# Graph attention on one Trainium2 core: one shared weight tile for the last chunk of six heads, 0/1 patterns for 17 of 22 chunks, and exponentials taken per node

## The chip, the core and the metric

The kernel runs on one core of a Trainium2 chip. The metric is device time in microseconds (us) of one execution, the median of several. The engines are named as in the profile: PE is the TensorE matrix engine (PEld its weight loads), DVE is VectorE, ACT is ScalarE, POOL is GpSimd, and SP is SyncE, which here only issues DMAs.

## The reference, cut to what matters

Four graph layers run one after the other on 2708 nodes with 512 features and a dense 0/1 adjacency of 2708 x 2708. Each layer is `x = x + layer(relu(layernorm(x)), adj)`. Only layer 2 is touched. It is masked attention with eight heads of 64 features:

```python
Wh = jnp.einsum('nd,hdo->hno', x, W)
f1 = jnp.einsum('hno,ho->hn', Wh, a1)
f2 = jnp.einsum('hno,ho->hn', Wh, a2)
e = jax.nn.leaky_relu(f1[:, :, None] + f2[:, None, :], negative_slope=ALPHA)   # 0.2
e = jnp.where(adj[None, :, :] > 0, e, NEG_INF)
attention = jax.nn.softmax(e, axis=-1)
h_prime = jnp.einsum('hnm,hmo->hno', attention, Wh)
out = jax.nn.elu(h_prime)
```

The kernel never forms `e`. For a node n and a neighbour m, exp(leaky(f1+f2)) equals e^(f2) * e^(0.2 f1) * max(e^(0.8 f1), e^(-0.8 f2)). The factor e^(0.2 f1) belongs to n alone and cancels in the softmax. So the kernel needs three things: `rb`, the row of e^(0.8 f1) over all n, the same on every partition; `ec`, one number e^(-0.8 f2) for each m; and `ef`, one number e^(f2) for each m, which is multiplied into the rows of Wh.

## The kernel before

**Chunks, units and steps.** The neighbours m are cut into NC = 22 chunks of R = 128 rows. The last one, chunk 21, has only 20 rows (`last_rows`). The columns n of one head are a *unit*. Heads 1 to 6 are whole units of 2708 columns (units 2 to 7). Head 0 is cut into two units of 1408 and 1300 columns (units 0 and 1), and so is head 7 (units 8 and 9). A *step* is one chunk of one unit: 10 x 22 = 220 steps, unit by unit, in each the chunks 0 to 21.

**What one step does.**

- `make` (L979) runs on DVE. One instruction gives the tile of weights t = max(rb, ec) * vT, where vT is the adjacency in bytes: 128 x 2708 numbers, or 20 x 2708 for the last chunk. The tiles t rotate through a ring of four buffers.
- `scale` (L967) runs on ACT. It makes the other operand, `whs` = Wh * ef (64 columns), and for most steps a second small tile for the sums of the weights (32 columns, L975).
- `multiply` (L1180) runs on PE. It adds t times whs into the PSUM tiles `av`, and into the PSUM tiles `sums` the sums of the weights, as float32 matmuls.
- `compare` (L996) and `multiply_sides` (L1195) replace those float32 sums in part of the steps. In units 2 to 8, for the chunks in the list `BY_SIDE`, ACT turns t into a bfloat16 pattern b of zeros and ones: a Sigmoid with the slope 2^62 says which side of the max was taken. PE multiplies b with small precomputed `parts`. The rest of the sum doesn't depend on the side, and is had from a count of neighbours that is made once for all heads.
- `mask` (L1250) and `count_neighbors` (L1258) make that count. For each chunk in `BY_SIDE` ACT casts the bytes of vT to bfloat16 in four pieces (tiles `x`, a ring of five that other tiles share), and PE multiplies them. These casts are laid among the steps of units 0 and 1, two steps for one chunk.
- `evict` (L1205) copies a finished unit from PSUM on ACT, and SP issues the DMAs to DRAM (`avT`, `sumT`).

`BY_SIDE` has 13 chunks before: `m % 5 in (1, 3, 4)`.

**Rows and exponentials.** f1 and f2 of all nodes lie in `f12`, nodes on partitions. `row2` (L1060) turns f1 of one chunk round on PE (`f_ps`), ACT copies it and issues its DMA to `rT` in DRAM. `load_row1` (L934) reads a row of rT back by DMA onto all 128 partitions (1354 KB for 2708 columns), and `exp_row` (L944) takes its exponential on ACT, once for each unit of the head, or half of it. `exps2` takes the exponentials `ef` and `ec`. `exp_nodes` (L1287) takes e^(0.8 f1) again in node layout into `er`, for layer 3. The calls of `row2` for chunks 0 to 16 and the first row of rb come with the dense product that ends before the attention (`rows2`, L1074). Those for chunks 17 to 21 come in the first steps of unit 0.

**Order of the work.** The program writes the steps in one loop (L1338): with step s it writes `scale` and `make` of step s+3, `compare` of step s+1, `multiply` of step s, `multiply_sides` of step s-1, and then what `plan` has for s, entered by `behind(step, function, ...)`. A scheduler then orders the instructions on each engine anew, within what the data and the rings allow, so the order on an engine can differ from the order of the program. [...]

Of the kernel before, what the change touches and what calls it, by code (L numbers as in the profile page):

```python
# [8 lines left out]
F32 = mybir.dt.float32  # L9
# [5 lines left out]
AF = mybir.ActivationFunctionType  # L15
ALU = mybir.AluOpType
# [4 lines left out]
P = 128  # L21

R = 128
# [7 lines left out]
SLOPE2 = 0.2  # L31
# [13 lines left out]
def fast_layers(  # L45
# [36 lines left out]
    nc = tc.nc  # L82
    N, D = x_in.shape
    H, _, O = w2.shape
    NC = -(-N // R)
# [3 lines left out]
    last_rows = N - (NC - 1) * R  # L89
    assert last_rows <= TAIL and TAIL + last_rows <= R  # L90

    def rows(c):
        return min(R, N - c * R)
# [18 lines left out]
    EARLY = NC // 2  # L112
# [14 lines left out]
    ident = const.tile([P, P], F32, name="ident")  # L127
# [274 lines left out]
    vT = []  # L402
# [5 lines left out]
    where = {c: (g, k) for g, cs in enumerate(groups) for k, c in enumerate(cs)}  # L408
# [481 lines left out]

    BY_SIDE = [m for m in range(NC) if m % 5 in (1, 3, 4)]


    STEEP = 2.0**62
# [5 lines left out]
    units[-1:] = [(H - 1, 0, cut), (H - 1, cut, N)]  # L902
    units[:1] = [(0, 0, cut), (0, cut, N)]
    assert all((hi - lo) % 4 == 0 for _, lo, hi in units)
    steps = [(u, m) for u in range(len(units)) for m in range(NC)]

    def by_side(u, m):
        return 1 < u < len(units) - 1 and m in BY_SIDE
# [6 lines left out]
    late = ctx.enter_context(tc.tile_pool(name="late", bufs=1))  # L915
    f12 = late.tile([P, NC, 2 * H], F32, name="f12")
    nc.gpsimd.memset(f12, 0.0)
    at_ctx = ctx.enter_context(ExitStack())
    at = at_ctx.enter_context(tc.tile_pool(name="att", bufs=1, reuse_waits="tile"))
    ef = at.tile([R, NC, H], F32, name="ef")  # L920
# [8 lines left out]
    one6 = at.tile([R, S], F32, name="one6")  # L929
    nc.gpsimd.memset(one6, 0.0)  # L930
    nc.gpsimd.memset(one6[:, 6:7], 1.0)
    row, weight, wh, whs, acc, sides, made, scaled = {}, {}, {}, {}, {}, {}, [], []

    def load_row1(h, lo, hi):  # L934

# [5 lines left out]
            bass.AP(tensor=src.tensor, offset=src.offset, ap=[[0, R], [1, hi - lo]]),  # L941
        )

    def exp_row(h, lo, hi):  # L944
        t = row[h][:, lo:hi]

        with tc.issue_after(scaled[-1]) if scaled else ExitStack():
            nc.scalar.activation(t, t, AF.Exp, scale=1.0 - SLOPE2)


    GROUP = 3

    def load_wh(s):
        u, m = steps[s]
        h = units[u][0]
        t = at.tile([R, GROUP, O], F32, name="wh", bufs=3)
        k = min(GROUP, NC - 1 - m)
        if k > 0:
            src = whd[m * R : (m + k) * R, h * O : (h + 1) * O]
            nc.sync.dma_start(t[:, :k], src.rearrange("(k p) o -> p k o", p=R))  # L960
        if k < GROUP and m + k == NC - 1:
            src = whd[(NC - 1) * R :, h * O : (h + 1) * O]
            nc.sync.dma_start(t[:last_rows, k], src)
        for j in range(GROUP):
            wh[u, m + j] = t[:, j]

    def scale(s):  # L967

        u, m = steps[s]
        h, q = units[u][0], rows(m)  # L970
        t = at.tile([R, O + S], F32, name="whs", bufs=4)
        by = ef[:q, m, h : h + 1]
        ins = nc.scalar.activation(t[:q, :O], wh.pop((u, m))[:q], AF.Copy, scale=by)  # L973
        if not by_side(u, m):
            nc.scalar.activation(t[:q, O:], one6[:q], AF.Copy, scale=by)  # L975
        whs[s] = t
        scaled.append(ins.ins)

    def make(s):  # L979
        u, m = steps[s]  # L980
        h, lo, hi = units[u]
        q = rows(m)
        g, k = where[m]
        t = at.tile([R, N], F32, name="t2", bufs=TILES)
        ins = nc.vector.scalar_tensor_tensor(  # L985
            t[:q, : hi - lo],
            row[h][:q, lo:hi],
            ec[:q, m, h : h + 1],
            vT[g][:q, k, lo:hi],
            op0=ALU.max,  # L990
            op1=ALU.mult,
        )
        weight[s] = t
        made.append(ins.ins)

    def compare(s):  # L996

        u, m = steps[s]
        h, lo, hi = units[u]
        q = rows(m)  # L1000
        if by_side(u, m):
            b = at.tile([R, N], BF16, name="b", bufs=2)
            nc.scalar.activation(  # L1003
                b[:q, : hi - lo],
                weight[s][:q, : hi - lo],
                AF.Sigmoid,
                bias=eb[:q, m, h : h + 1],
                scale=STEEP,
            )
            sides[s] = b  # L1010
# [48 lines left out]

    def row2(c):  # L1060
        pf = ps.tile([P, R], F32, name="f_ps", tag="ps")
        nc.tensor.transpose(pf[:H], f12[:R, c, :H], ident[:R, :R])
        r = at.tile([H, R], F32, name="row", bufs=2)
        nc.scalar.copy(r, pf[:H])
        nc.scalar.dma_start(rT[:, c * R : (c + 1) * R], r)

    def exps2(cs):
        nc.scalar.activation(ef[:, cs], f12[:R, cs, H:], AF.Exp)
# [1 line left out]


    LATE = NC - 5

    def rows2(c):  # L1074
        if c < LATE:
            row2(c)
        if c == EARLY - 1:
            load_row1(*units[0])

        if c == LATE:  # L1080
            exps2(slice(0, EARLY))
            exp_row(*units[0])
            load_wh(0)
            load_wh(GROUP)
        if LATE < c <= LATE + 3:
            scale(len(made))
            make(len(made))
# [5 lines left out]
    staged(NC, *stages2, done=len(AHEAD))  # L1093
    l2p.close()

    e3_ctx = ctx.enter_context(ExitStack())
    e3 = e3_ctx.enter_context(tc.tile_pool(name="e3", bufs=2, side="right", reuse_waits="tile"))
    er = e3.tile([R, NC, H], F32, name="er", bufs=1)
    kept3, l3_weights = {}, []


# [77 lines left out]

    def multiply(s):  # L1180
        u, m = steps[s]
        q = rows(m)
        half, quarter = sizes_of(u)
        if m == 0:
            acc[u] = [
                [ps.tile([P, 512], F32, name=name, tag="ps") for _ in pieces(w)]
                for name, w in (("av", half), ("sums", quarter))
            ]
        t, w = weight.pop(s)[:q], whs.pop(s)[:q]
        cols = [w[:, a : a + S] for a in range(0, O + S, S)]  # L1190
        four(acc[u][0], half, [(cols[j % 2], t, j // 2) for j in range(4)], s)
        if not by_side(u, m):
            four(acc[u][1], quarter, [(cols[2], t, j) for j in range(4)], s)
# [26 lines left out]
    def split():  # L1220

        nc.scalar.mul(eb, ec, -STEEP * ABOVE)
        rest = common.tile([P, D], F32, name="rest", tag="t", bufs=3)
        rest = rest[:R, : NC * H].rearrange("p (m h) -> p m h", h=H)
        for i in range(2):
            e = ef
            if i:
                nc.vector.tensor_tensor(rest, ec, ef, ALU.mult)
                e = rest
            for k in range(3):  # L1230
                part = parts_of[:, :, :, 3 * i + k]
                nc.scalar.copy(part, e)
                if k < 2:
                    nc.vector.tensor_tensor(rest, e, part, ALU.subtract)
                    e = rest
        for i, heads in enumerate((slice(1, H), slice(1, H - 1))):
            for r in sorted({m % 5 for m in BY_SIDE}):
                ms = [m for m in BY_SIDE if m % 5 == r]
                src = parts_of[:, r :: 5, heads, 3:6]
                at_i = [BY_SIDE.index(m) for m in ms]  # L1240
                nc.scalar.copy(parts2[:, at_i[0] : at_i[-1] + 1 : 3, i, heads], src)


    fourths = [0, cut // 2, cut, (cut + N) // 2, N]
# [39 lines left out]
                    sumT[7 * H :, fourths[j] + a : fourths[j] + b], t[own, : b - a]  # L1284
                )

    def exp_nodes():  # L1287
        nc.scalar.activation(er, f12[:R, :, :H], AF.Exp, scale=1.0 - SLOPE2)
        nc.sync.dma_start(er[TAIL : TAIL + last_rows, NC - 1], er[:last_rows, NC - 1])

    def load_l3_weights():
# [6 lines left out]
    def behind(s, fn, *args):  # L1298
        plan.setdefault(s, []).append((fn, args))

    for c in range(LATE, NC):
        behind(c - LATE + 1, row2, c)
    behind(4, exps2, slice(EARLY, NC))
    behind(5, load_row1, *units[1])
    behind(6, exp_row, *units[1])
    behind(9, split)
    behind(30, load_l3_weights)
    behind(30, exp_nodes)
    for u in range(2, len(units)):
        if units[u][1] == 0:  # L1310
            s = max(1, u - 1) * NC
            behind(s + 2, load_row1, units[u][0], 0, N)
            behind(s + 9, exp_row, units[u][0], 0, N)
    for u in range(len(units)):
        behind((u + 1) * NC - 1, evict, u, 0)
        behind(min((u + 1) * NC, len(steps) - 1), evict, u, 1)
    for i in range(len(BY_SIDE)):
        for j in range(4):
            behind(11 + 2 * i + j // 2, mask, i, j)
        behind(13 + 2 * i, count_neighbors, i)  # L1320

    for at_step, fn, c in (
        (16, load3, 0),
# [12 lines left out]
        behind(len(steps) - at_step, fn, c)  # L1336

    for s in range(len(steps)):  # L1338
        if s + 6 < len(steps) and (s + 6) % NC % GROUP == 0:
            load_wh(s + 6)  # L1340
        if s + 3 < len(steps):
            scale(s + 3)
            make(s + 3)
        if s + 1 < len(steps):
            compare(s + 1)
        multiply(s)
        multiply_sides(s - 1)
        for fn, args in plan.pop(s, ()):
            if fn in (load_l3_weights, exp_nodes, split):
                with tc.issue_after(made[s]):  # L1350
                    fn(*args)
            else:
                fn(*args)
# [740 lines left out]
```

## Time and profile before

| what | value |
|---|---|
| median of three runs | 1788.5 us (1788.35 to 1793.66) |
| the profiled execution's own time | 1790.6 us |
| its span in the trace | 1788.8 us (1.8 us lie around it) |
| granted TensorE clock, mean | 0.996 |
| PE busy | 1763.6 us, 99% of the span |
| DVE busy | 1306.7 us, 73% |
| ACT busy | 818.2 us, 46% |
| attention, first to last step on PE | from 830.23 us to about 1380 us of the span |
| unit 1 / 2 / 3 / 8 / 9 begins on PE at | 873.12 / 913.88 / 978.03 / 1305.83 / 1339.79 us |

All durations below come from the one profiled execution. Times are counted from the start of its span. A row of the groups names the line of the code, the engine, the operation, the tile that is written and the tiles that are read, how often it ran, its busy time and the mean of one in ns, and then the engine's idle time just before these instructions with what ended most of it. Busy rows give a digit for each fortieth of the span: 9 is 90% or more.

### The profile page before, as it was taken

Reading aid. Unit: us, or ns where it says so; the run is one execution under the profiler, and the core shown is the slowest. Engines: PE = TensorE matmul, PEld = TensorE weight load, DVE = VectorE, ACT = ScalarE, POOL = GpSimd, SP = SyncE. Lnnn points to the kernel's source line nnn. Section 1 sums busy time; section 2 is a strip of 40 time slices with the busy share of each in tenths; the row PEclk is TensorE's granted clock in tenths of the full one; section 3 lists DMA queues with packets and bytes.
Section 4 is the critical chain, followed back from the end, with each engine's and each line's share of the span. In section 5 each row is a group of like instructions: output and inputs, shape, how many; then the busy total and the mean of one; then the engine's idle time right before and its main releaser. Section 6 shows DMA issues by size and latency. Waiting matters only on the chain.

```text
span 1788.8 us, 30688 instructions
## 1 busy us (share of the span) xinstructions
PE 1763.6 (99%) x11880; PEld 1042.3 (58%) x11880; DVE 1306.7 (73%) x1834; ACT 818.2 (46%) x1561; POOL 251.0 (14%) x251
## 2 busy tenths in 40 slices
PE   8999999999999999999999999999999999999998
PEld 5567777744458888644544344444344455588786
DVE  7648777855456556889899999999998777633334
ACT  5447666712210000265977767777774566400000
POOL 0003322311111111365000000000001222100000
PEclk9999999999999999999999999999999999999999
DMA  8436665534451111343221122022022444312221
GB/s 294 132 100 205 195 200 165 157 98 122 120 150 47 48 48 50 118 129 126 60 60 44 28 61 58 14 63 59 15 68 68 130 141 135 99 54 88 71 71 40
DMA packets 166399, 175.80 MB, mean 98 GB/s; under 512 B 83535, under 2 KB 105999, under 8 KB 165348
## 3 DMA queue, kind: packets, MB, share of 16 engines
q1 hardware_dynamic: 143596, 130.35, 26.1%
q10 hardware_dynamic: 18808, 33.37, 4.9%
q0 software_dynamic: 3840, 10.03, 1.4%
q8 instruction: 95, 1.56, 0.3%
q14 instruction: 60, 0.49, 0.1%
HBM read 110.34 MB, written 55.36 MB: 93 GB/s over the span
## 4 chain that ended last, share of the span: by engine, by line
PE 90%; DVE 6%; issue 2%; DMA 2%; ACT 1%; POOL 0%; SPq 0%; DVEq 0%; POOLq 0%; ACTq 0%
PE acc L423 35%; PE av L1172 19%; PE nb_ps L186 8%; PE sums L1172 6%; PE h_ps L186 4%; PE wh_ps L186 4%; PE self_ps L186 4%; PE line_ps L186 4%; DVE t L985 3%; PE hT_ps L244 2%; PE fused_ps L369 2%; DVE cum L552 1%; DMA degd<-deg 1%; PE sums_ps L615 1%; PE av_ps L1125 1%
## 5 line engine op out<-in xcount | busy, mean ns | idle before, releaser
L985 DVE SCALAR_TENSOR_TENSOR t<-rb,ec,vT 128x2708 f32<-128x2708 f32 (+2 forms) x220 | 529.6, 2462 | 13.2 <-PE sums L1172 8.6
L1172 PE MATMUL av<-t,whs 128*32 128x451 f32 (+3 forms) x4576 | 436.9, 516 | 0.9 <-DVE ln_mv L220 0.9
L423 PE MATMUL acc<-halves,kt 128*128 128x512 f32 x1848 | 433.3, 394 | 2.4 <-DVE kt L839 2.1
L423 PEld LDWEIGHTS acc<-halves,kt 128*128 128x128 f32 x1848 | 345.8, 188 | 86.0 <-DVE kt L839 6.7
L1172 PEld LDWEIGHTS av<-t,whs 128*32 128x32 f32 (+1 forms) x4576 | 160.4, 110 | 205.1 <-issue 177.9
L423 PE MATMUL acc<-halves,ar 128*128 128x512 f32 x924 | 244.6, 414 | 0.0
L1003 ACT ACTIVATE b<-t,eb 128x2708 bf16<-128x2708 f32 (+3 forms) x91 | 218.1, 2396 | 28.0 <-DVE t L985 27.3
L423 PEld LDWEIGHTS acc<-halves,ar 128*128 128x128 f32 x924 | 170.7, 188 | 55.1 <-issue 13.8
L839 DVE SCALAR_TENSOR_TENSOR kt<-lastr,index,vT 128x512 fp32r<-128x512 int16 (+3 forms) x154 | 111.4, 735 | 75.8 <-PE acc L423 75.4
L222 ACT ACTIVATE ln_rs<-ln_mv,eps 128x1 f32<-128x1 f32 x88 | 25.6, 293 | 302.1 <-DMA x<-x 200.3
L1411 DVE CAST kt<-vT 128x512 fp32r<-128x512 uint8 (+3 forms) x154 | 56.5, 368 | 138.0 <-PE acc L423 138.0
L1139 POOL TENSOR_SCALAR z<-y 128x512 f32<-128x512 f32 x22 | 44.1, 2004 | 657.7 <-DVE y L1132 648.9
L1172 PE MATMUL sums<-t,whs 128*32 128x338 f32 (+4 forms) x1464 | 131.0, 448 | 2.5 <-ACT out L1213 2.5
L552 DVE TENSOR_TENSOR_SCAN cum<-ai,deg 128x512 int16<-128x512 int32 (+2 forms) x110 | 128.2, 1178 | 0.0
L973 ACT ACTIVATE whs<-wh,ef 128x64 f32<-128x64 f32 x220 | 76.6, 348 | 108.3 <-PE sums L1172 50.2
L580 ACT ACTIVATE cum<-cum,limit 128x512 int16<-128x512 int16 (+3 forms) x132 | 87.9, 666 | 49.4 <-DVE deg L560 48.9
L1172 PEld LDWEIGHTS sums<-t,whs 128*32 128x32 f32 (+1 forms) x1464 | 53.1, 109 | 64.7 <-issue 38.5
L218 DVE BATCH_NORM_STATS2 ln_st<-x 128x6 f32<-128x512 f32 x88 | 60.2, 685 | 36.0 <-DMA x<-x 22.1
L186 PE MATMUL nb_ps<-wfn,hT 128*128 128x512 f32 x168 | 78.8, 613 | 2.1 <-ACT hT L246 2.1
L186 PE MATMUL h_ps<-w0s,hT 128*128 128x512 f32 x168 | 76.0, 595 | 0.0
L186 PE MATMUL wh_ps<-w2s,hT 128*128 128x512 f32 x168 | 75.8, 593 | 0.0
L186 PE MATMUL self_ps<-wfs,hT 128*128 128x512 f32 x168 | 75.6, 592 | 0.0
(201 smaller groups left out, 1893.9 us busy)
## 6 DMA issues: line engine op xcount, KB each, us to landing
x<-x SPq DMA_DIRECT2D x105, 256.0 KB
ai<-in_adj SPq DMA_DIRECT2D x84, 256.0 KB
x<-x ACTq DMA_DIRECT2D x84, 256.0 KB
x<-in_x SPq DMA_DIRECT2D x42, 256.0 KB
rb<-rT SPq DMA_DIRECT2D x7, 1354.0 KB
wh<-whd SPq DMA_DIRECT2D x70, 96.0 KB
packed<-two POOLq DMA_DIRECT2D x44, 128.0 KB, 3.6
whd<-wh SPq DMA_DIRECT2D x21, 256.0 KB
```

Of the source, the lines that this page charges most:

```text
L186: nc.tensor.matmul(po[:n], lhsT[:, f, :n], w[:, f, :], start=(f == 0), stop=(f == NF - 1))
L218: nc.vector.bn_stats(st[:n], xc[:n])
L423: nc.tensor.matmul(acc[:R], weight[:, k * R : (k + 1) * R], parts[:, i, :], start=(m == 0 and i == 0), stop=(m == NC - 1),)
L552: nc.vector.tensor_tensor_scan(cum[:n, :gw], ai[:n, :gw], ai[:n, :gw], 0.0 if g == 0 else deg[:n, m : m + 1], op0=ALU.add, op1=ALU.max,)
L580: nc.scalar.activation(cum[:n, :gw], cum[:n, :gw], AF.Sign, bias=limit[:n], scale=-1.0, accum_out=signs[:n, m, g : g + 1],)
L839: nc.vector.scalar_tensor_tensor(by_chunk(kt, cs), lastr[:, cs[0] * R : (cs[-1] + 1) * R].rearrange("p (c r) -> p c r", r=R), index[:R, m ...
L973: ins = nc.scalar.activation(t[:q, :O], wh.pop((u, m))[:q], AF.Copy, scale=by)
L985: ins = nc.vector.scalar_tensor_tensor(t[:q, : hi - lo], row[h][:q, lo:hi], ec[:q, m, h : h + 1], vT[g][:q, k, lo:hi], op0=ALU.max, op1=AL ...
L1003: nc.scalar.activation(b[:q, : hi - lo], weight[s][:q, : hi - lo], AF.Sigmoid, bias=eb[:q, m, h : h + 1], scale=STEEP,)
L1139: nc.gpsimd.tensor_scalar(z, y, 0.0, None, op0=ALU.min)
L1172: nc.tensor.matmul(p[j * S : (j + 1) * S, : b - a], lhsT, rhs[:, part * size + a : part * size + b], start=(s % NC == 0), stop=(s % NC == ...
L1411: nc.vector.tensor_copy(by_chunk(kt, cs), pattern(m, cs))
```

## The change

1. **The last chunk of heads 1 to 6 in one tile.** Six heads have 20 rows each in chunk 21, which is 120 lines. `load_tails` collects them by 30 DMAs on SP (for each head: its row of rT onto 20 partitions, the bytes of vT, f2, and its rows of Wh with the small columns for the sums) into the tiles `tails_row`, `tails_v`, `tails_f` and `tails_w`. `exp_tails` (three instructions on ACT) and `make_tails` (one on DVE) make from them one tile of weights for all six. In units 2 to 7 chunk 21 has no `make` and no `scale` any more: `multiply` takes the whole tile of 120 lines with weights that are zero outside the head's own 20. Units 2 to 8 now begin with chunk 21.
2. **More patterns.** `BY_SIDE` has 17 chunks: all but 2, 7, 12, 17 and 21. The four casts of a chunk come every 7/4 steps in place of every 2.
3. **Exponentials in node layout.** `er` = e^(0.8 f1) is taken before the row is turned round (`exps_nodes`), so that rT holds exponentials already. The eight `exp_row` on the broadcast rows go. `row2` is called for chunks 0 to 10 in the dense stage, two at a time, and for 11 to 21 in steps 4 to 9 of unit 0. The row of unit 1 is loaded behind step 10 in place of step 5.
4. **The pool `e3`** of layer 3 is opened at step 155, when the tails' pool is closed.

```diff
-    BY_SIDE = [m for m in range(NC) if m % 5 in (1, 3, 4)]
+    BY_SIDE = [m for m in range(NC - 1) if m % 5 != 2]
...
-    steps = [(u, m) for u in range(len(units)) for m in range(NC)]
+    middle = [units[u][0] for u in range(2, len(units) - 2)]
+
+    def in_tails(u, m):
+        return m == NC - 1 and units[u][0] in middle
+
+    steps = [
+        (u, m)
+        for u in range(len(units))
+        for m in ((NC - 1, *range(NC - 1)) if 1 < u < len(units) - 1 else range(NC))
+    ]
...
-    def exp_row(h, lo, hi):
-        t = row[h][:, lo:hi]
-
-        with tc.issue_after(scaled[-1]) if scaled else ExitStack():
-            nc.scalar.activation(t, t, AF.Exp, scale=1.0 - SLOPE2)
-
+    LINES = len(middle) * last_rows
...
+    def load_tails():
+        g, k = where[NC - 1]
+        for i, h in enumerate(middle):
+            own = lines_of(h)
+            src = rT[h : h + 1, :N]
+            nc.sync.dma_start(
+                tails_row[own],
+                bass.AP(tensor=src.tensor, offset=src.offset, ap=[[0, last_rows], [1, N]]),
+            )
+            nc.sync.dma_start(tails_v[own], vT[g][:last_rows, k, :N])
+            nc.sync.dma_start(tails_f[own, :1], f12[:last_rows, NC - 1, H + h : H + h + 1])
+            nc.sync.dma_start(
+                tails_w[own, i, :O], whd[(NC - 1) * R :, h * O : (h + 1) * O]
+            )
+            nc.sync.dma_start(tails_w[own, i, O:], one6[:last_rows])
+
+    def exp_tails():
+        f = tails_f[:LINES]
+        nc.scalar.activation(f[:, 1:2], f[:, :1], AF.Exp)
+        nc.scalar.activation(f[:, 2:3], f[:, :1], AF.Exp, scale=SLOPE2 - 1.0)
+        nc.scalar.activation(tails_w[:LINES], tails_w[:LINES], AF.Copy, scale=f[:, 1:2])
+
+    def make_tails():
+        nc.vector.scalar_tensor_tensor(
+            tails_row[:LINES],
+            tails_row[:LINES],
+            tails_f[:LINES, 2:3],
+            tails_v[:LINES],
+            op0=ALU.max,
+            op1=ALU.mult,
+        )
...
     def scale(s):
...
+        if in_tails(u, m):
+            whs[s] = tails_w[:LINES, middle.index(h)]
+            return
...
     def make(s):
...
+        if in_tails(u, m):
+            weight[s] = tails_row[:LINES]
+            made.append(made[-1])
+            return
...
     def row2(c):
         pf = ps.tile([P, R], F32, name="f_ps", tag="ps")
-        nc.tensor.transpose(pf[:H], f12[:R, c, :H], ident[:R, :R])
+        nc.tensor.transpose(pf[:H], er[:, c], ident[:R, :R])
...
+    def exps_nodes(cs):
+        nc.scalar.activation(er[:, cs], f12[:R, cs, :H], AF.Exp, scale=1.0 - SLOPE2)
+
...
     def rows2(c):
-        if c < LATE:
-            row2(c)
-        if c == EARLY - 1:
+        for first, end in early_rows:
+            if c == end - 1:
+                exps_nodes(slice(first, end))
+            for n in range(2):
+                if first <= first + 2 * (c - end + 1) + n < end and c >= end - 1:
+                    row2(first + 2 * (c - end + 1) + n)
+        if c == EARLY + 1:
             load_row1(*units[0])
 
         if c == LATE:
             exps2(slice(0, EARLY))
-            exp_row(*units[0])
...
-    for c in range(LATE, NC):
-        behind(c - LATE + 1, row2, c)
+    behind(4, exps_nodes, slice(EARLY, NC))
     behind(4, exps2, slice(EARLY, NC))
-    behind(5, load_row1, *units[1])
-    behind(6, exp_row, *units[1])
+    for c in range(EARLY, NC):
+        behind(4 + (c - EARLY) // 2, row2, c)
+    behind(10, load_row1, *units[1])
     behind(9, split)
+    behind(12, load_tails)
+    behind(18, exp_tails)
+    behind(22, make_tails)
     behind(30, load_l3_weights)
-    behind(30, exp_nodes)
+    behind(30, spread_nodes)
     for u in range(2, len(units)):
         if units[u][1] == 0:
-            s = max(1, u - 1) * NC
-            behind(s + 2, load_row1, units[u][0], 0, N)
-            behind(s + 9, exp_row, units[u][0], 0, N)
+            behind(max(1, u - 1) * NC + 2, load_row1, units[u][0], 0, N)
...
     for i in range(len(BY_SIDE)):
+        first = 11 + 7 * i // 4
         for j in range(4):
-            behind(11 + 2 * i + j // 2, mask, i, j)
-        behind(13 + 2 * i, count_neighbors, i)
+            behind(first + j // 2, mask, i, j)
+        behind(first + 2, count_neighbors, i)
...
     for s in range(len(steps)):
+        if s == (len(units) - 3) * NC + 1:
+            tails_ctx.close()
+            e3_ctx = ctx.enter_context(ExitStack())
```

## The prediction

> **What bounds the kernel now.** I read the page first: the rows by slice tell which engines are full where.
>
> ```profile
> PE 1763.6 (99%) x11880; PEld 1042.3 (58%) x11880; DVE 1306.7 (73%) x1834; ACT 818.2 (46%) x1561; POOL 251.0 (14%) x251
> ...
> PE   8999999999999999999999999999999999999998
> ...
> DVE  7648777855456556889899999999998777633334
> ACT  5447666712210000265977767777774566400000
> ```
>
> One slice is 44.7 us, so the attention is slices 19 to 31. PE is full everywhere; in the attention DVE is too, ACT only around slice 20. Outside it the change leaves the work alone. So I went on with the table of windows (columns: window, length, busy time of PE, PEld, DVE, ACT, POOL with instructions, granted clock, DMA share, GB/s): end of unit 0 with unit 1, unit 2, unit 3, and one unit's period.
>
> ```profile
> 857.50:914.00 56.50, 55.41 (x828) 31.29 (x820) 48.32 (x30) 52.71 (x120) 0.00 (x0) 1.00 0.20 53
> 914.00:978.00 64.00, 64.00 (x768) 27.27 (x765) 64.00 (x23) 47.22 (x49) 0.00 (x0) 1.00 0.13 35
> 978.00:1047.00 69.00, 66.51 (x780) 26.84 (x776) 68.47 (x24) 49.40 (x53) 0.00 (x0) 0.98 0.18 51
> 1174.10:1238.80 64.70, 64.70 (x782) 27.57 (x784) 64.70 (x23) 48.00 (x53) 0.00 (x0) 1.00 0.16 44
> ```
>
> The reader is to see that a middle unit takes 64.7 us, and that PE and DVE are both busy for all of it: a tie. Shortening PE alone gains nothing; ACT has 16 us to spare. In units 0 and 1 it is ACT that is short (52.7 of 56.5). Unit 3 is longer, and the chain of waits says why:
>
> ```profile
> 973.92 5.98 DVE t L985 x2
> ...
> 979.99 2.55 ACT b L1003
> 982.54 0.43 ACT out L1213
> ...
> 983.01 1.81 PE sums L1172 x24
> ```
>
> The new unit's sums need PSUM banks that are freed by an eviction; on ACT it stands behind a Sigmoid, and that behind the tile from DVE. PE idles 2.5 us. Last, the groups of the middle units (window 923 to 1303) and ACT's order in unit 0:
>
> ```profile
> L985 DVE SCALAR_TENSOR_TENSOR t<-rb,ec,vT 128x2708 f32<-128x2708 f32 x122 | 360.5, 3023 | 0.5 <-PE sums L1172 0.3 <-PE av L1172 0.2
> ```
> ```profile
> 857.92 2.71 ACT L1256 CAST x<-vT 128x704 bf16<-128x704 uint8 x4
> 860.54 0.34 ACT L973 ACTIVATE whs<-wh,ef 128x64 f32<-128x64 f32 x1
> ```
>
> A make starts every 360.5/122 = 2.955 us, and DVE waits 0.5 us in 360: DVE paces units 2 to 7. (Columns: line, engine, operation, tiles, shapes, count; busy time, mean ns; idle time before, with releasers.) One cast costs 2.71/4 = 0.67 us.
>
> **The change, part by part.** Times are of the profiled execution (1790.6 us; its span of 1788.8 and 1.8 around it). "Order" below is the order in which the built program's instructions stand on each engine's queue.
>
> *Dense stage and steps 0 to 13.* Six of 17 f_ps transposes leave the dense stage (a wh_ps pair takes 3.98 us with one and 3.87 without: -0.7), and five more than before come into unit 0 (a step takes 2.12 with one and 1.77 without: +1.8). Sum +1.1. Two more table loads (1.28 each) stand on ACT in the dense stage; it is busy 34.3 of 60 us there, and before its loads stopped PE nowhere: nothing. On ACT, exp_tails and the five more row copies add some 3.3 us where it idles 12 of 27.5 us: nothing; uncovered, 3.3.
>
> *Casts.* 17 x 4 = 68 casts in place of 52: 16 x 0.67 = 10.7 us more on ACT, where it is the short engine. The order makes it worse than the sum. Between the scale of step 17 (859.6, with the 1.1) and that of step 22 stand 30 casts: 20.0; 5.5 pairs of scale at 0.5: 2.8; three evictions: 1.2. Eighteen of these casts and the evictions lie in one block just before the scale of step 22. So step 22's scale comes at about 883.6, while PE ends step 21 near 874 and has only counts to do: it idles some 9 us. Unit 1 begins at 883.6 in place of 873.1: +10.4.
>
> *Unit 1.* 22 x 1.64 + 8.25 counts x 0.29 = 38.5, and 1 for waits: 39.5 in place of 40.8: -1.3. [...] Row: after the 2.5 us gap at 980.5 the first 3.41 us of matmuls ran at half speed, which lost 1.7. [...] I take 2.0. Unit 2 thus begins 10.4 - 1.3 + 2.0 = 11.1 later, at 925.0.
>
> *Units 2 to 8.* PE loses four float32 sums per unit for bfloat16 ones: 4 x (1.14 - 0.29) = 3.4, to 61.3. DVE loses one of 22 makes: 21 x 2.955 = 62.0. DVE is the bound, so 2.7 per unit is what is had. Before, DVE began unit 2's makes 4.9 ahead of PE. The same lead gives: -4.9 + 6 x 21 x 2.955 (372.3) + 22 half makes at 1.595 (35.1) + the first make of unit 9 and its handover (1.55 + 0.8) = 404.9 from unit 2's start to unit 9's. I add 1.5 for unit 2's first Sigmoids, behind eight copies of the counts (3.6) and a table load (1.3): 406.4. Before it was 1339.8 - 913.9 = 425.9: -19.5. ACT per middle unit: 17 x 2.55 + 21 x 0.25 + 4 x 0.25 + evictions 2.3 = 52 of 62: it fits, because exp_row (2.46) and its two table loads leave. The boundary stall (2.5 us and half clock) costs PE 4.4, which DVE's pace covers.
>
> *Tails.* make_tails has 120 lines; makes of 20 and of 128 lines both take 3.02, so 3.0. It stands on DVE after four makes of unit 1, where DVE waits for PE: nothing; if not, 3.0. Its cover is PE's idle. The 30 DMAs go on SP ahead of unit 1's row and Wh: 24 small ones at the 0.30 to 0.48 us that SP's issues take, about 10 us, end near 858 with the rest, their data near 864. Step 22 has its scale only at 883.6: covered. The six rows are 1.27 MB: the 1.35 MB row before landed in about 5.5 us at up to 309 GB/s, so 5 us. [...]
>
> *End.* DVE leads PE by less at unit 9, where layer 3's first vector work comes in: +0.5, between 0 and 2.
>
> Sum: 11.1 - 19.5 + 0.5 = -7.9: 1782.7 for the profiled execution. The median of the runs is 2.1 below that execution, so **1780.6 us**.
>
> **Rivals.**
> 1. *The casts cost little* (chance 0.13). Were the block broken up on the chip, ACT's 10.7 us would be spread over units 0 and 1, where 3.8 us are free and unit 1's exp_row (2.46) leaves: unit 2 would begin 4 later instead of 11: 1773.5. For it: the sum alone says so. [...]
> 2. *ACT stays short through unit 1* (0.20). From 883.6 it has 33 casts (22.0), 22 pairs of scale (11.0), copies and evictions (4.5): 37.5 of 39.5. The casts wait for a ring of five tiles that PE empties; at 0.2 to 0.4 us for each cast, or with DVE's lead lost at unit 2 (4.9), unit 2 and its end come 5 to 12 later: 1785.5 to 1792.5, no change. For it: the block itself. Against: before, DVE kept its lead through such a stretch.
> 3. *Slower: SP's queue* (0.08). Unit 1's row stands on SP behind 32 small DMAs. SP starts on them near 835 and must have issued the row by 878 for it to land by 883.6. So this decides from 43/32 = 1.34 us for one. If the small pieces (4 bytes to 128 bytes for each line) take 2 us each, [...]the row is issued at 899 and lands at 905: 21 later than step 22 otherwise begins, less the casts that are done meanwhile (some 4): +17 - 7.9 = +9, 1797.5. Even follows from about 1.6 us each. For it: nothing before shows 4-byte pieces. Against: sumT's eight small ones take 2.81, 0.35 each.
> 4. *The change doesn't do what it says* would show as 22 makes in a unit; the built order has 21.
>
> **How the numbers follow.** About 0.3% (5.4 us) is what a measurement of this kernel can tell from no change: below 1783.1 is faster, above 1793.9 slower. The likeliest case (0.59) spans 1775.5 to 1785 by its unknowns ([...]tails 0 to 3, start lead, end 0 to 2), a tenth of it above 1783.1. Faster: 0.53 + 0.13 + 0.02 from rival 2 = 0.68. Slower: 0.08, with nothing of rival 2: 0.08. Same: 0.24. The range of 8 in 10, 1772 to 1788.5, leaves out rival 3, the upper half of rival 2 and some of rival 1's far end.
>
> **What would show it.** Right: a PE gap of some 9 us ending near 883.6 with a row of casts on ACT under it; unit 2's first step near 925; makes 2.95 apart with no idle from there on and a period of 62.0; unit 9 near 1331. Wrong: unit 1 beginning before 878 (rival 1), DVE idle in units 2 to 7 (ACT or PE would be the bound), or a step 22 that waits for rb (rival 3).

## The result, and the profile after

The changed kernel took 1778.8 us (median of 4 runs, 1777.8 to 1782.6), the kernel before 1789.1 beside it. The ratio is 0.9942, with a 95% interval of 0.9927 to 0.9957: faster by 0.4 to 0.7%. The forecast was 1780.6. The profiled execution is the longest of the four (1782.6, span 1780.8), so between the two traces the gain is 8.0 us, and between the medians 10.3. These are the lines of its page that the prediction showed of before:

```profile
PE 1750.7 (98%) x11704; PEld 1042.6 (59%) x11704; DVE 1289.9 (72%) x1829; ACT 850.4 (48%) x1553; POOL 249.3 (14%) x252
...
PE   8999999999999999999999999999999999999998
...
DVE  7648787854446555888789999999999777633334
ACT  5447666722210000265788887888794666400000
```

PE lost 12.9 us of work and DVE 16.8, while the span lost only 8.0. ACT has 32 us more. Where the time went is read from the first matmul of each unit on PE:

| stretch of the trace | before | after | difference | forecast |
|---|---|---|---|---|
| start to the first attention step | 830.2 | 833.5 | +3.3 | -0.7 |
| unit 0 | 42.9 | 58.0 | +15.1 | +11.1 |
| unit 1 | 40.8 | 39.7 | -1.0 | -1.3, and +2.0 for the clock |
| units 2 to 8 | 425.9 | 403.2 | -22.7 | -19.5 |
| unit 9 and layer 3 | 449.0 | 446.3 | -2.7 | +0.5 |
| sum | 1788.8 | 1780.8 | -8.0 | -7.9 |

Of the 3.3 at the start, 2.8 is there already when layer 2's product begins (745.28 and 748.08), ahead of anything that the change touches. Nine more profiles of changed kernels, below, put the first attention step between 830.5 and 833.1, and what follows unit 9's start at 445.0 to 448.2. So the first row is mostly what executions differ by. In the last row the trace of before (449.0) lies above all ten traces of changed kernels; a small part of that difference may belong to the change, and no run here tells it apart.

**Unit 0 and the block of casts.** Two lines of the windows of after (the first spans the end of unit 0 with unit 1, the second is one middle unit), then ACT's timeline (start, duration, engine, line, operation, tiles; in brackets the idle time ahead and what ended it), and last two lines of SP's timeline:

```profile
857.50:925.00 67.50, 63.22 (x843) 34.67 (x839) 51.11 (x33) 59.06 (x141) 0.00 (x0) 0.95 0.35 86
1052.71:1114.66 61.95, 61.52 (x753) 24.81 (x744) 61.95 (x22) 50.98 (x48) 0.00 (x0) 1.00 0.17 47
```
```profile
875.05 2.73 ACT L1322 CAST x<-vT 128x704 bf16<-128x704 uint8 x4
880.92 2.05 ACT L1322 CAST x<-vT 128x704 bf16<-128x704 uint8 x3 [3.14 <-PE sums L1235]
...
883.56 1.46 ACT L1322 CAST x<-vT 128x704 bf16<-128x704 uint8 x2
884.92 0.46 ACT L1275 COPY out<-sums 128x352 f32<-128x352 f32 x1
885.27 5.99 ACT L1322 CAST x<-vT 128x650 bf16<-128x650 uint8 x9
891.16 0.59 ACT L1020 ACTIVATE whs<-wh,ef 128x64 f32<-128x64 f32 x2
```
```profile
862.85 2.66 SPq L966 DMA_DIRECT2D tails_row<-rT  x6
865.61 0.39 SPq L1006 DMA_DIRECT2D wh<-whd  x1
```

The scale of step 22 (891.16) comes behind 18 casts, and without a pause: it was not waiting for data, its turn in the queue came late. The rows of Wh that it needs were issued on SP at 865.61, behind the six broadcasts of the tails' rows. PE's last step of unit 0 began at 880.89, the first of unit 1 at 891.56. After that last step there is nothing on PE but counts, most of them waiting for casts. By the steps, unit 0's +15.1 is: +2.2 up to step 14, +2.3 at step 15 (taken back by 0.3), +2.4 at step 21, +8.5 at step 22. Of the 2.4 about 2.0 belongs to this one execution: PE stood still for 1.4 us in step 20, as no other profile has it (last section). skip_make, a run below whose program is the same up to unit 2, begins unit 1 at 56.0 and unit 2 at 95.8 after the attention's first step, where this trace has 58.0 and 97.8. So without the disturbance units 0 and 1 lose 12.1 us and not 14.1, and the difference of the spans would be about 10.0, near the 10.3 of the medians.

**The middle units.** The second window is unit 4, from its first matmul to the next unit's: 61.95 us, DVE busy in all of it (64.70 before). PE is idle for 0.4 of it. The group of the makes in the middle (window 940 to 1290), and PE's waits there (total us, times, longest):

```profile
L1035 DVE SCALAR_TENSOR_TENSOR t<-rb,ec,vT 128x2708 f32<-128x2708 f32 x120 | 354.1, 3027 | 0.0
```
```profile
PE av L1235 <- DVE t L1035: 1.4, 8, 0.2
```

354.1/120 = 2.951 us per make and no idle at all. PE now waits for DVE's tiles, 0.2 us at a time; the boundary stall of 2.5 us (PE sums behind an eviction) is no longer there.

**The clock.** Windows of after across the block (us, PE, PEld, DVE, ACT, POOL, granted clock, DMA share, GB/s):

```profile
880.00:885.00 5.00, 4.06 (x51) 1.19 (x44) 3.64 (x3) 4.08 (x8) 0.00 (x0) 0.89 0.14 29
885.00:888.00 3.00, 2.76 (x9) 0.39 (x8) 2.45 (x1) 3.00 (x7) 0.00 (x0) 0.50 0.53 130
888.00:891.00 3.00, 3.00 (x11) 0.49 (x10) 0.00 (x0) 3.00 (x5) 0.00 (x0) 0.54 0.77 209
891.00:894.00 3.00, 2.84 (x39) 1.29 (x41) 0.52 (x1) 3.00 (x10) 0.00 (x0) 1.00 0.75 284
```

The clock fell to half, but during the block, where PE had only counts to do (9 and 11 matmuls in 3 us); when unit 1 began it was back.

### The profile page after: what moved, and what is told of

Its sections match the earlier page's. It is cut to its first block, busy times and chain, and to the rows that moved or that the text cites. A ratio compares the mean times of both kernels' runs of the same rounds, so it can differ in the third digit from the quotient of the medians.

```text
span 1780.8 us, 30232 instructions
## 1 busy us (share of the span) xinstructions
PE 1750.7 (98%) x11704; PEld 1042.6 (59%) x11704; DVE 1289.9 (72%) x1829; ACT 850.4 (48%) x1553; POOL 249.3 (14%) x252
## 4 chain that ended last, share of the span: by engine, by line
PE 79%; DVE 11%; issue 4%; DMA 2%; ACT 2%; POOL 0%; SPq 0%; ACTq 0%; DVEq 0%; POOLq 0%
PE acc L423 35%; PE av L1235 14%; PE nb_ps L186 8%; DVE t L1035 8%; PE h_ps L186 4%; PE self_ps L186 4%; PE line_ps L186 4%; PE sums L1235 4%; PE hT_ps L244 2%; PE fused_ps L369 2%; PE wh_ps L186 2%; DMA x<-x 1%; DMA degd<-deg 1%; PE av_ps L1188 1%; ACT b L1053 1%
## 5 line engine op out<-in xcount | busy, mean ns | idle before, releaser
L1035 DVE SCALAR_TENSOR_TENSOR t<-rb,ec,vT 128x2708 f32<-128x2708 f32 (+2 forms) x214 | 510.9, 2448 | 17.1 <-PE sums L1235 15.5
L1235 PE MATMUL av<-t,whs 128*32 128x451 f32 (+5 forms) x4432 | 430.1, 514 | 5.7 <-DVE t L1035 1.4
L1053 ACT ACTIVATE b<-t,eb 128x2708 bf16<-128x2708 f32 (+1 forms) x119 | 285.1, 2396 | 36.4 <-DVE t L1035 36.3
L1484 DVE CAST kt<-vT 128x512 fp32r<-128x512 uint8 (+3 forms) x154 | 56.5, 368 | 137.3 <-PE acc L423 137.3
L1020 ACT ACTIVATE whs<-wh,ef 128x64 f32<-128x64 f32 x214 | 72.8, 344 | 53.1 <-PE sums L1235 18.6
L1235 PE MATMUL sums<-t,whs 128*32 128x325 f32 (+4 forms) x952 | 91.9, 448 | 0.0
L246 ACT ACTIVATE hT<-hT_ps 128x512 f32<-128x512 f32 x88 | 52.3, 594 | 58.6 <-PE hT_ps L244 54.4
L186 PE MATMUL nb_ps<-wn,hT 128*128 128x512 f32 x168 | 76.9, 601 | 0.0
```

What stands on the lines that cost most here:

```text
L186: nc.tensor.matmul(po[:n], lhsT[:, f, :n], w[:, f, :], start=(f == 0), stop=(f == NF - 1))
L246: evicted.append(nc.scalar.activation(hT[:, :, :n], pt[:, :, :n], AF.Relu).ins)
L1035: ins = nc.vector.scalar_tensor_tensor(t[:q, : hi - lo], row[h][:q, lo:hi], ec[:q, m, h : h + 1], vT[g][:q, k, lo:hi], op0=ALU.max, op1=AL ...
L1053: nc.scalar.activation(b[:q, : hi - lo], weight[s][:, : hi - lo], AF.Sigmoid, bias=eb[:q, m, h : h + 1], scale=STEEP,)
L1235: nc.tensor.matmul(p[j * S : (j + 1) * S, : b - a], lhsT, rhs[:, part * size + a : part * size + b], start=(s % NC == 0), stop=(s % NC == ...
L1484: nc.vector.tensor_copy(by_chunk(kt, cs), pattern(m, cs))
```

## The experiments

My theory after the result: in the middle PE and DVE were tied, so that only both parts together shorten a unit; and the loss in unit 0 is one of order, a scale put behind casts, more than of ACT's added work. Rivals: one of the two parts makes the gain alone; the 16 added casts cost their time wherever they stand.

### Each part alone

**Shared tile with 13 patterns** (tails_13):

```diff
-    BY_SIDE = [m for m in range(NC - 1) if m % 5 != 2]
+    BY_SIDE = [m for m in range(NC - 1) if m % 5 in (0, 1, 3)]
...
-        first = 11 + 7 * i // 4
+        first = 11 + 2 * i
```

> The changed kernel with 13 patterns in place of 17 (chunks with m % 5 in 0, 1, 3), so the shared tile is there but PE keeps nine float32 sums per unit. Theory (PE and DVE were tied, so both parts are needed): PE is the bound, 13 x 2.57 + 9 x 3.41 = 64.1 us per middle unit; the middle gains 0 to 4 against before, while units 0 and 1 still lose about 12 to 14: 1793 to 1801, slower than before. Rival (DVE alone paces the middle units, the pattern count doesn't matter): 62.0 per unit as in the changed kernel, and about 1779 or less, as 16 casts are gone.

**17 patterns without the shared tile** (pat_17):

```diff
     def in_tails(u, m):
-        return m == NC - 1 and units[u][0] in middle
+        return False
...
-    behind(12, load_tails)
-    behind(18, exp_tails)
-    behind(22, make_tails)
```

> The changed kernel without the shared tile: chunk 21 is made, scaled and loaded for every head, and the 30 DMAs are gone; 17 patterns stay. Theory: DVE is the bound at 22 x 2.955 = 65.0 us per middle unit although PE needs only 61.3; units 2 to 8 take about 422, 3 to 4 less than before (the boundary stall is covered). In ACT's built order the block of casts before step 22 is gone, so units 0 and 1 lose only 4 to 6: together 1787 to 1792, no change to before. Rival (PE's 3.4 per unit count by themselves): about 61.5 per unit, 1768 to 1772.

Measured: tails_13 1790.1 us, ratio to before 0.9997 (0.9988 to 1.0005); pat_17 1789.7 us, 0.9998 (0.9989 to 1.0006). Neither part alone changes the time. A middle unit of tails_13 with DVE's waits in its middle units, and then a unit of pat_17:

```profile
1015.40:1079.50 64.10, 64.10 (x780) 48.48 (x776) 62.07 (x22) 42.37 (x48) 0.00 (x0) 1.00 0.17 46
```
```profile
DVE t L1035 <- PE av L1235: 9.5, 5, 2.1
```
```profile
1047.20:1112.10 64.90, 64.64 (x744) 25.01 (x744) 64.90 (x23) 51.66 (x51) 0.00 (x0) 0.95 0.16 46
```

With 13 patterns PE is full for 64.10 us and DVE waits for it; with 22 makes DVE is full for 64.90. (PE's granted clock was 0.95 in that unit, but DVE has no wait at all in the middle units of pat_17, so DVE sets this period.) Both are the periods that the expectation named (64.1 and 65.0), and both rivals (62.0 and 61.5) are out. The tie of before was thus not exact: PE alone needs 64.1, DVE alone 64.9, and a unit took 64.7. The time of tails_13 was expected 3 to 11 us longer. It still had the block (unit 1 began 54.3 us after the attention's first step, 42.9 before), but unit 1 was 2.9 shorter than before and units 2 to 8 took 418.7 in place of 425.9: the middle gained 7.2, since before's boundary stall is gone, where I had allowed 0 to 4. Most of it is unit 3, 4.9 shorter. Units 0 and 1 lost 8.6, where I had expected 12 to 14. pat_17 came within its 1787 to 1792: units 2 to 8 took 421.0 (422 expected), and units 0 and 1 lost 5.3 (4 to 6 expected). That neither changed the time by so much as 0.1% is partly luck: in tails_13 a gain of 7.2 in the middle meets a loss of 8.6 ahead of it, in pat_17 4.9 meets 5.3. What the tie itself shows is the unit's period, which falls by no more than 0.6 in either run.

### One more make taken away

skip_make tells whether 61.95 is DVE's figure or a coincidence:

```diff
+        if m == NC - 2 and h in middle:
+            weight[s] = weight[s - 1]
+            made.append(made[-1])
+            return
```

> The changed kernel, but in units 2 to 7 chunk 20 takes chunk 19's tile of weights again in place of its own (so its part of the sums is left out of the computation): 20 makes per unit, everything else as it was. Theory (DVE's makes pace the middle units at 21 x 2.95 = 61.95, PE has slack): the units fall to PE's own need, 22 x 2.28 + 5 x 1.14 + 17 x 0.29 = 60.8, perhaps 61.2 with waits at the boundaries; six units give 4 to 7 us: 1772 to 1775. Rival (61.95 is set by something else, PE's waits at the unit boundary or ACT's Sigmoids): the units stay at 61.5 to 62, 1777.5 to 1779.

Measured: 1773.7 us, ratio 0.9910 (0.9893 to 0.9926). A unit, and DVE's waits in the middle:

```profile
1047.96:1108.68 60.72, 60.72 (x752) 45.65 (x744) 59.06 (x21) 51.05 (x48) 0.00 (x0) 1.00 0.18 49
```
```profile
DVE t L1039 <- PE av L1239: 7.9, 5, 1.7
```

The unit falls to 60.7, PE is full and DVE waits for it; unit and time are as the theory had them. So in the changed kernel DVE paces the units, and PE's own need, 1.2 us below, is the next bound.

### The block: order or work

**Row DMAs later** (rows_22): all casts stay; the six broadcasts of the tails' rows are issued later, and with them make_tails, which needs them.

```diff
+    def load_tail_row(i):
+        src = rT[middle[i] : middle[i] + 1, :N]
+        nc.sync.dma_start(
...
-    behind(22, make_tails)
+    for i in range(len(middle)):
+        behind(22 + 2 * i, load_tail_row, i)
+    behind(36, make_tails)
```

> The changed kernel, but the six DMAs that broadcast the tails' rows are issued behind steps 22, 24, ... 32 in place of step 12, and make_tails behind step 36. All 68 casts stay. Theory (the wait at step 22 comes from the order: Wh of step 22 stood on SP behind the six row DMAs, so its scale was put behind 18 casts on ACT): the block is gone, unit 2 begins 8 to 10 us earlier, and the time is 1768 to 1772. Rival (ACT is simply short by the 16 extra casts, and what isn't paid before unit 1 is paid inside it): unit 2 begins at most 3 earlier, 1775 to 1779.

**Tails loaded one head at a time** (spread_20):

```diff
-    behind(12, load_tails)
-    behind(18, exp_tails)
-    behind(22, make_tails)
+    for i in range(len(middle)):
+        behind(20 + 3 * i, load_tails, (i,))
+    behind(38, exp_tails)
+    behind(40, make_tails)
```

> The changed kernel, but the tails of one head at a time are loaded (its 5 DMAs) behind steps 20, 23, ... 35, exp_tails behind 38 and make_tails behind 40. Theory: as the run with only the rows moved, and the wait of 1.0 us on ACT for tails_f with the instructions queued behind it (casts that begin 2.3 later) goes as well: 1766 to 1771, up to 2 less than that run. Rival for the second part (the 2.3 is no loss of its own, since ACT's casts set the pace anyway): the same as that run within 1 us. Rival for the whole: 1775 to 1779.

Measured: rows_22 1775.2 us, ratio to before 0.9913 (0.9899 to 0.9926); spread_20 1774.4 us, 0.9909 (0.9894 to 0.9925). The ACT timeline of rows_22 at the same place:

```profile
874.42 0.35 ACT L1023 ACTIVATE whs<-wh,ef 128x64 f32<-128x64 f32 x1 [0.16 <-PE sums L1238]
874.67 0.30 ACT L1025 ACTIVATE whs<-one,ef 128x32 f32<-128x32 f32 x1
874.89 2.71 ACT L1325 CAST x<-vT 128x704 bf16<-128x704 uint8 x4
877.51 0.34 ACT L1023 ACTIVATE whs<-wh,ef 128x64 f32<-128x64 f32 x1
```

Step 22 is scaled at 874.42, with four casts behind it in place of 18 ahead. On SP, Wh of step 22 now stands behind one row in place of six (864.39). Counted from the attention's first step, unit 1 begins at 47.9 in place of 58.0, or of the undisturbed 56.0: 8.2 earlier. But unit 1 then takes 42.7 in place of 39.7, so unit 2 begins only 5.2 earlier (90.6 and 95.8). The window of unit 1 shows why:

```profile
881.00:924.00 43.00, 41.48 (x625) 35.07 (x621) 37.39 (x22) 42.24 (x96) 0.00 (x0) 1.00 0.24 71
```

ACT is busy for 42.2 of 43.0 us. So theory and rival each have a part of it. The block was a matter of order: it goes with all 68 casts left in, here and in pat_17, which has no tails to load and scales step 22 at 39.8 after the attention's first step. But of the 12.1 us that units 0 and 1 lose in the changed kernel only 5.2 were order; 3.0 of what was won in unit 0 came back inside unit 1, where ACT is nearly full. The start of unit 2 lies between theory (8 to 10 earlier) and rival (at most 3), and the time, 1775.2, lies outside the theory's 1768 to 1772 and just inside the rival's 1775 to 1779. Order was worth 3.6 us by the two medians, and 5.2 by the two ratios to before.

The second part of spread_20 was not put to the test. In its trace the rows are issued later, but 23 of the 24 small DMAs still stand on SP from 839.0 to 862 and the first two instructions of exp_tails still run just ahead of the casts (862.4): the scheduler had moved them forward again. Its first cast stands 31.6 us after the attention's first step, as in the changed kernel (31.3) and in rows_22 (31.4). Its time (1774.4) missed the 1766 to 1771, and is within 1 us of rows_22.

**The small DMAs on POOL's queue** (tails_poolq), the block left in:

```diff
-            nc.sync.dma_start(tails_v[own], vT[g][:last_rows, k, :N])
-            nc.sync.dma_start(tails_f[own, :1], f12[:last_rows, NC - 1, H + h : H + h + 1])
+            nc.gpsimd.dma_start(tails_v[own], vT[g][:last_rows, k, :N])
+            nc.gpsimd.dma_start(tails_f[own, :1], f12[:last_rows, NC - 1, H + h : H + h + 1])
...
```

> The changed kernel (1778.8), but the 24 small DMAs of the tails are issued on POOL's queue in place of SP's; ACT's built order keeps its block of 19 casts before step 22. Theory (the small DMAs cost 0.72 us each on SP, so tails_f arrived late and held ACT's queue, casts behind it, by about 2): 1776 to 1777.5. Rival (ACT would have waited anyway, the block decides): 1778.3 to 1779.5. Third: POOL's queue is slower for them, tails_f is later still: over 1779.5.

Measured: 1777.9 us, ratio 0.9936 (0.9923 to 0.9950), between theory and rival and not to be told from the changed kernel's 0.9942. In its trace the first cast comes 30.1 after the attention's first step, 1.2 earlier, and unit 2 comes at 95.0, 2.8 earlier. But about 2.0 of that is the disturbance of the changed kernel's own profile; against skip_make (95.8) it is 0.8. So the small DMAs cost about 1 us in unit 0. pat_17, without them, agrees: its first cast comes at 29.9, 1.4 before the changed kernel's.

### Less work for ACT

**One cast in four on POOL**, on top of rows_22 (rows_22_pool), and **16 patterns**, on top of rows_22 (rows_22_16):

```diff
-        nc.scalar.copy(t[:q, : own.stop - own.start], vT[g][:q, k, own])
+        eng = nc.gpsimd.tensor_copy if j == 3 else nc.scalar.copy
+        eng(t[:q, : own.stop - own.start], vT[g][:q, k, own])
```
```diff
-    BY_SIDE = [m for m in range(NC - 1) if m % 5 != 2]
+    BY_SIDE = [m for m in range(1, NC - 1) if m % 5 != 2]
```

> The run with the rows moved (1775.2), and in addition the last of each chunk's four casts is made on POOL, which is idle there. ACT was busy for 42.2 of 43.0 us of unit 1 in that run; it loses 17 casts of about 0.65 = 11 us. Theory (with the block gone, ACT's sum of casts is what holds units 0 and 1): unit 2 begins 4 to 6 earlier, up to where PE is full, 1769 to 1772. Rival (a cast on POOL is slow, or slows DVE's makes beside it, so that counts or tiles come later): no gain or a loss, 1775 to 1780. Nearest row for POOL's price: 2.0 us for 128 x 512 float32, which would make 17 x 2.5 = 43 us of some 65.

> The run with the rows moved, with 16 patterns (chunk 0 back to float32 sums): four casts and some copies less on ACT. Theory (DVE is the bound of the middle at 62.0; PE at 16 patterns needs 22 x 2.28 + 6 x 1.14 + 16 x 0.29 = 61.6): the middle stays at 61.95 per unit and units 0 and 1 get 2 to 3 us back: 1772 to 1773.5. Rival (PE's stall at the unit boundaries no longer fits under DVE's pace): up to 1 us more per unit, 1775 to 1779.

**Both queues relieved** (rows_pool_q): rows_22_pool with the small DMAs on POOL's queue as well.

> The rows moved, one cast in four on POOL, and the 24 small DMAs of the tails on POOL's queue, all together. The earlier runs showed: the end follows from DVE's first make of unit 2 (it came 92.5 us after the attention's first step in the changed kernel, 85.4 with the rows moved, 84.3 with POOL's casts). Theory: the small DMAs off SP let ACT's casts begin some 2 us earlier in unit 0, PE is full in unit 1, so that make comes at 82 to 83.5 and the time is 1770.5 to 1773. Rival (DVE's own makes and make_tails hold unit 1 now): 84.3 again, 1773 to 1775.

Measured: rows_22_pool 1773.8 us, 0.9912 (0.9898 to 0.9926); rows_22_16 1773.9 us, 0.9910 (0.9895 to 0.9925); rows_pool_q 1773.6 us, 0.9911 (0.9894 to 0.9927). By the medians none of them can be told from rows_22 or spread_20; the five lie within 1.6 us, and all three miss the times that the theory named. The traces can tell them apart. POOL's casts in rows_22_pool cost (group of window 855 to 930) and unit 1 looks like this:

```profile
L1326 POOL CAST x<-vT 128x650 bf16<-128x650 uint8 x16 | 23.5, 1471 | 50.7 <-PE adj_sums L1338 43.0 <-ACT whs L1023 4.4 <-ACT whs L1025 3.3
```
```profile
881.00:924.00 43.00, 43.00 (x641) 30.61 (x636) 40.92 (x22) 38.28 (x84) 15.07 (x10) 1.00 0.25 68
```

A cast on POOL takes 1.47 us, twice ACT's (0.73 for this shape in the same run), and PE is full for all of unit 1. Unit 2 begins 87.2 us after the attention's first step in place of 90.6 in rows_22: 3.4 earlier, where 4 to 6 were expected. Yet unit 8 begins only 1.1 earlier. The reason is seen in DVE's timeline, at its first make of unit 2. All figures are counted from the attention's first step, from the traces:

| kernel | DVE's first make of unit 2 | PE begins unit 2 | PE begins unit 8 | from that make to unit 8 |
|---|---|---|---|---|
| changed kernel | 92.5 | 97.8 | 467.1 | 374.6 |
| rows_22 | 85.4 | 90.6 | 459.9 | 374.6 |
| spread_20 | 86.2 | 91.4 | 460.8 | 374.6 |
| rows_22_16 | 85.4 | 90.3 | 460.2 | 374.8 |
| rows_22_pool | 84.3 | 87.2 | 458.8 | 374.6 |
| rows_pool_q | 83.1 | 86.0 | 457.6 | 374.6 |

126 makes at 2.951 are 371.8, and 2.8 follow until PE has the last tile worked off: the last column is DVE's chain, whatever PE does ahead of it. Where unit 2 begins earlier on PE than DVE is ready for, unit 2 takes longer (61.73 in rows_22_pool, 60.46 in rows_22). In rows_22_16 a middle unit takes 61.56, PE's own need with one more float32 sum (I had reckoned 61.6), and eats DVE's lead until the last two, at 61.80 and 62.07. The first make itself came no earlier there than in rows_22: the four casts that were saved are the last of unit 1, and its first make doesn't wait for them. That expectation failed on the 2 to 3 us for units 0 and 1. rows_pool_q brought the make to 83.1, inside the 82 to 83.5 that was expected, but the time (1773.6) lies above the 1770.5 to 1773; its span is 1770.8 where the changed kernel's is 1780.8.

So of the 12.1 us that units 0 and 1 lose, 5.2 go with the order (rows_22), another 4.6 when work is taken from ACT's and SP's queues (rows_pool_q, unit 2 at 86.0), and 2.4 stay, about what unit 0 has lost by step 14 through the f_ps that moved into it.

## Why the prediction was right, and where it was not

The time (1780.6 forecast, 1778.8 measured), the sign and the mechanism were right: DVE's makes pace the middle, and a block of casts ahead of one scale costs part of that gain. Point by point:

- **DVE paces the middle, 21 makes of 2.955.** Right: 61.95 per unit, with no idle on DVE. Each part alone shortens the unit by no more than 0.6, as a tie of two engines says, and taking one make more away moves the bound to PE. PE's own need is 60.7, not the 61.3 of the prediction, which took 3.4 from the full 64.7.
- **Units 2 to 8 in 406.4.** Measured 403.2. The largest of the terms that were mis-sized is the 1.5 added for unit 2's first Sigmoids: nothing was lost there. The lead at unit 2 was 5.2 in place of 4.9 (0.3), the pace 2.951 in place of 2.955 (0.5 over 126 makes), and the rest, some 0.8, lies in unit 8 and the handover to unit 9.
- **The block before step 22.** Right in kind, place and size: 18 casts and three evictions ahead of one scale. That the built order would hold on the chip was assumed; the trace has it so at this place, with the 30 casts between the two scales and 18 of them in the block. From the scale of step 17 to that of step 22 the sum had 24.0 us; skip_make, undisturbed, has 24.7 (the changed kernel's trace 26.7). Counted from its start unit 0 was to lose 11.1; it lost 15.1, and 13.1 in skip_make. What the sum lacked is +2.3 at step 15: PE's queue has the first counts ahead of that step, and they waited for ACT's casts, which began at 31.3 after the attention's first step (27.7 before). The f_ps that moved into unit 0 explain 2.2 of these 3.6 (the prediction had +1.8 for them), as pat_17 shows with 29.9; the other 1.4 came with the tails, which the prediction had put at nothing: there was idle time on ACT, but not where the queue stood waiting (0.99 us for `tails_f`, up to 859.60). Its start for this sum, 859.6, was also misread: the scale of step 17 stands at 857.45 in before, and 858.6 with the 1.1.
- **ACT as the short engine in units 0 and 1.** The row that was read for it (ACT 52.7 of 56.5 us) has PE busy for 55.4. Before, PE was the fuller engine there.
- **The clock, +2.0 at unit 1.** Wrong: 0. The 2.0 was my estimate, from a loss of 1.7 by the row. The row that it leaned on was also misread. After the gap of 2.5 us that ends at 983.0, the window 982.9 to 984.5 still has a granted clock of 1.00, and 984.5 to 988.1 has 0.53: the half speed began 1.6 us after the first matmul, not with it. In the changed kernel the half speed lay inside the block (883.9 to 890.7), where PE had nothing to do but counts. Steps of unit 1 took 1.64 from the second on.
- **Small DMAs.** I took SP's 0.30 to 0.48 for one. SP's timeline in after has 0.71 to 0.82 for three of the four kinds and 0.43 to 0.50 for the fourth. Three of them:

```profile
857.68 0.71 SPq L971 DMA_DIRECT2D tails_f<-f  x1
858.45 0.49 SPq L972 DMA_DIRECT2D tails_w<-whd  x1
858.99 0.73 SPq L975 DMA_DIRECT2D tails_w<-one  x1
```

  The 24 took some 16 us, not 10. That is far from the 1.34 for one from which rival 3 would have decided, and cost about 1 us. (By rival 3's own figures its break-even is 1.7, not 1.6; its 2 us for one were assumed, and no trace shows them.)
- **The six row DMAs.** I took 5 us, by the row of before that goes to 128 partitions, and with it a landing ahead of make_tails. The window in which they run almost alone:

```profile
870.00:880.00 10.00, 8.62 (x124) 5.87 (x119) 7.39 (x5) 7.63 (x16) 0.00 (x0) 1.00 0.62 101
```

  The DMA share is 0.62 and the rate 101 GB/s, where the 128-partition row of before reached 0.92 and 309 (window 851 to 853). 1.27 MB at 101 GB/s take about 13 us, as an estimate from this row. They were done by 882, ahead of make_tails at 884.4. That it cost nothing was owed to the block: with unit 1 in time, make_tails would have stood near 876 and waited for them. That is argued, not shown.
- **The rivals.** Rival 2 (ACT short all through unit 1) is true of rows_22, not of the changed kernel, where PE paced unit 1 (39.7). Rival 1 (the casts cost little) is what the runs with the rows moved approach: unit 2 begins 90.6 - 83.7 = 6.9 after before's, in place of 14.1 (12.1 undisturbed).

The sum agreed with the trace (-7.9 and -8.0) better than it should have: the loss in units 0 and 1 was 2.3 larger than forecast (14.1 against 11.8 with the clock), the gain of the middle 3.2 larger, and the two ends 0.8 worse. Some 2.0 of that loss is the disturbance, which happened to hide most of what the middle gained beyond the forecast; that agreement is luck. Without it units 0 and 1 come to 12.1, close to 11.8, but there too two errors cancel: +2.0 for a clock that cost nothing, and nothing for the late casts.

Left open: how much of what the tails cost at ACT's first casts is the issue of the small DMAs and how much exp_tails. tails_poolq, whose small DMAs are on POOL's queue, still runs exp_tails ahead of the casts, and begins them at 30.1, close to pat_17's 29.9, which points to the DMAs.

## What to carry to other kernels

Where two engines are both full over a stage, look for the smaller of the two savings, and expect nothing from one alone: here each half shortened a middle unit by 0.6 us or less, and both by 2.7. Look in the queues' built order for what stands ahead of the first operation of the next unit, since a late load can put it behind work that could wait; moving six DMAs past it gave 3.6 us by the medians. But expect part of that back where the engine is nearly full anyway: here 3.0 of 8.2 us. Look in the trace, too, whether an edit of the program's order reached the queues: in spread_20 the scheduler undid it for 23 of the 24 small DMAs. And of two engines in a chain, count from the first instruction of the slower one: what the faster one gains ahead of it comes back as a longer unit (here unit 2 took 61.73 us in rows_22_pool and 60.46 in rows_22).

## What the hardware showed that was not expected

The changed kernel's profile has a wait on PE that no other run shows, with no releaser; it lies in step 20, and what stands behind it in the queue is late with it:

```profile
879.30 0.49 PE L1235 MATMUL av<-t,whs 128*32 128x352 f32 x3 [1.38 <-issue]
```

ACT's casts, behind PE's counts, waited 3.14 us at the same time. skip_make, alike up to there, begins step 21 at 45.3 after the attention's first step, the changed kernel at 47.4. The profiled execution (1782.6) is also 3.8 over the median of its kernel. One more thing in the trace stands out at that place. The queue q8, of the kind "instruction", moves packets of 16 KB, 94 in this profile, with 256 instructions of PE and its weight loads between two of them at the median. One starts at 857.3 and the next only at 876.4, after 499 such instructions, the most between two packets here (the next most is 370), with the six row broadcasts under way in between. PE's last weight load ahead of the wait starts at 877.2, while that packet is still under way (until 877.6), and PE goes on at 879.3. In skip_make the same packet comes 403 instructions after the one before it, and PE doesn't wait. No run here shows whether the wait has to do with that packet.

Broadcasts of a DRAM row onto 20 partitions moved at a third of the rate of one onto 128 (101 and 309 GB/s), though the DMA share fell only from 0.92 to 0.62; no run here shows why. And a granted clock that fell where PE had little to do cost nothing here, since it was back by the first matmul of unit 1: it was 0.50 and 0.54 in the block, and 1.00 from 891 on.
